# First loads of the modulation's rows queued behind loads of h, with shifted ranks and one scaling moved to GpSimd

## The chip, the cores and the metric

The kernel runs on one core of a Trainium2 chip. The metric is device microseconds (us) of one execution. In the text PE is TensorE (matmul), DVE is VectorE, ACT is ScalarE, POOL is GpSimd, and SP is SyncE, which here only issues DMA transfers. All transfers of this kernel are issued from SP, one after the other, in the order of the program; a transfer that has to wait for something holds up those behind it in that queue.

## The reference

The input x has 128 sequences of 64 tokens with 256 values each (8192 tokens), and `cond_1024` has one row of 256 values for each sequence. Two layers follow one another:

```python
x = x + _L0_ffn_ref(_L0_cond_ref(cond_1024, x, W, b, alpha), clip_x, clip_down, w_gate, w_up, w_down)
x = x + _L1_ffn_ref(_L1_cond_ref(x, cond_1024[:, None, :], w_q, ..., w_ada, b_ada), weight, bias)
```

`_L0_cond_ref` is a gated recurrence over the 64 time steps. `_L0_ffn_ref` is a feed-forward block with values rounded to 8 bits: `h = silu(gate) * up` is rounded with one scale for the whole tensor, so its largest absolute value must be known before any of it can be used. `_L1_cond_ref` is a transformer block in hyperbolic space, modulated by the condition:

```python
ada = t_emb @ w_ada + b_ada
sh_msa, sc_msa, g_msa, sh_mlp, sc_mlp, g_mlp = jnp.split(ada, 6, axis=-1)
xn = layer_norm(logmap0(x))
xm = expmap0(xn * (1 + sc_msa) + sh_msa)          # then attention with 16 heads of 16 values
attn_t = g_msa * logmap0(attn_out)
x = mobius_add(residual, expmap0(attn_t))
xn = layer_norm(logmap0(x))
xm = expmap0(xn * (1 + sc_mlp) + sh_mlp)          # then two products, w_f1 and w_f2
ff_t = g_mlp * logmap0(ff)
return mobius_add(residual, expmap0(ff_t))
```

`_L1_ffn_ref` rounds its input in blocks of 32 to a 6-bit format and multiplies it by a weight.

## The kernel before, in words

**First phase (0 to about 301 us).** The scan runs over 64 steps. Beside it the weights are prepared, and the six modulation vectors of all 128 sequences are computed and stored to DRAM as `ada_d`, eight copies of each row. Then `h_chunk` computes h in 16 blocks of 512 tokens and stores it to `h_d` and `hr_d`. L556 to L561 take the largest absolute value and derive the scale `cu`; L561 is the last DVE instruction of the phase.

**Second phase, `fused`.** The 8192 tokens are 64 tiles of 128, two tiles are a pair, and four tiles are a group; there are 16 groups. The loop at the end of `fused` is a software pipeline over turns k from -5 to 18. In turn k it writes down:

- `tail(k)`: the sums and coefficients after attention of group k and after the MLP of group k-3 (`chain.tail`, from L790), then `comb.a` and `comb.m` (L835), which add the residual; `comb.a` also feeds the statistics (L732, L733) of the second normalisation;
- `norms(k)`: the normalisation coefficients (`chain.ln`; `rnln` and `lnaln` at L666), then `modulate` (L751 to L756) for the MLP of group k and for the attention of group k+5, and `clip_ball`, which scales each tile by `sur` (L653 on DVE, L655 on POOL; `CFG['su0']` and `CFG['su1']` name the engine for each of the four tiles of a group, V for DVE and G for POOL);
- `fp6(k-3)`, `mlp(k)` and `attention(k+5)`;
- `front(k+6)`: for each of two pairs it rounds h to 8 bits (`front.q8`, L655 with `hb`), casts it (L913, L915), multiplies (`front.mm`, L925), scales (`front.x1`, L928), adds x (`front.add`, L930, with `xr` from DRAM), and stores the result in `x1_d`. It also issues the load of h for a pair two further on (`load_h`), because there are two buffers `hl`.

**Rows of the modulation.** `load_ada(which, kind, n_, i)` loads rows of `ada_d` for tile i. `which` is 0 for attention and 1 for the MLP; `kind` 0 loads shift and scale together (256 KB), `kind` 2 the gate (128 KB). The tiles are called ada00, ada02, ada10 and ada12, with 2, 2, 2 and 4 buffers. Their memory, like all of the second phase's work tiles, is that of the first phase's tiles, so no such load can start before the first phase has ended. The two `hl` buffers lie elsewhere, and pairs 0 and 1 of h are loaded while the first phase still runs.

**Order.** The text of the program doesn't set the order on an engine. Each instruction gets a priority, and a planner with a simulated clock goes through them: on each engine the ready instruction with the smallest priority comes first. The priority is set by

```python
tc.cur_priority = base + (turn_[0] + LA) * TURN + RANK[name]
```

with TURN = 1800, so a difference of 1800 in `RANK` is a whole turn. `tc.issue_after(ins)` adds an edge: instructions on the same engine as `ins` that are written inside the block come behind `ins` in that engine's order; no semaphore is added.

Of the kernel before, what the change touches and what calls it, by code (L numbers as in the profile page):

```python
# [22 lines left out]
P = 128  # L23
B, T, D = 128, 64, 256
# [18 lines left out]
NG = NT // GN  # L43
AR = 8
TS = 4
CFG = {'rnd': 'S', 'ef': 8, 'hold': [3, 0], 'mk': 2, 'raw': 1, 'mv': 6, 'xs': 3, 'la': 3, 'sb': 7, 'qks': 'GGGG', 'deq': 'VV', 'first': 1000, 'hb': 2, 'q_h': 'P', 'q_x1': 'P', 'q_xr': 'P', 'q_ot': 'P', 'q_out': 'P', 'q_ada': 'P', 'room': [[0.3, 0.3, 0.55], [0.5, 0.4, 0.2]], 'qv': 64, 'p1': 'GVGVGVGV', 'x1': 3, 'u1': 16, 'u2': 6, 'qkv': 2, 'sq': 1, 'uT1': 2, 'uT2': 2, 'qM': 2, 'kT': 2, 'e': 4, 'oT': 1, 'yT': 1, 'hq': 2, 'hl': 2, 'xr': 1, 'ot': 2, 'ada00': 2, 'ada02': 2, 'ada10': 2, 'ada12': 4, 'dn': 1, 'qk': 2, 'sc': 2, 'ao': 1, 'ml': 1, 'fp': 1, 'mod0': 'GGGV', 'mod1': 'VVVV', 'sqm0': 'SSSS', 'sqm1': 'SSSS', 'su0': 'VVVV', 'su1': 'VGVG', 'q8': 'GGGGGG', 'hqc': 'SSSVVV', 'qm': 'SSSS', 'x1a': 'GV', 'gate0': 'GGGG', 'gate1': 'GGGG', 'yb': 'GG', 'va': 'GGGG', 'sqt': 'SSSS', 'sqg': 'SSSS', 'sqo': 'SSVS', 'f2e': 'SSSS', 'early': 0, 'q8f': 'VVVVVV', 'hqf': 'SSSVVV', 'fl': 1, 'un': 2, 'jsu': 1, 'LA': 5, 'LM': 3, 'tl': 6, 'ord': 1, 'xt': 3, 'q_xt': 'P', 'fill': {'x1a': 'V', 'mod0': 'V'}}
GT = 4
NGR = NTILE // GT

TURN = 1800  # L50
RANK = {"front.q8": -307, "front.cast": 756, "front.mm": -718, "front.x1": -1025, "front.add": 4029, "store.x1": 0, "a.turn": -1220, "a.hi": -574, "a.lo": -1296, "a.qkv": 62, "a.qkvcopy": -226, "a.sq": 2196, "a.nh": -44, "chain.h": -3529, "a.qk": -90, "a.va": -90, "a.turnq": -90, "a.qm": -1303, "a.kt": -1196, "a.sc": -90, "a.e": -1043, "a.av": -90, "a.raw": -1317, "a.o": 3284, "a.turno": 1510, "a.ot": -3205, "a.wo": 975, "a.proj": -2819, "m.turn": 1039, "m.hi": -1145, "m.lo": -1565, "m.mm": 1778, "m.dot": -447, "m.copy": 619, "m.a": -39, "f.max": -10785, "f.q": 4848, "f.rnd": -1723, "f.deq": 2715, "f.turn": 765, "f.yt": 4647, "f.mm": 799, "load.ot": 10309, "f.add": -562, "store.out": 280, "x2n": 2132, "own": -510, "load.xt": -607, "chain.su": 3853, "chain.full": -6602, "chain.cf": 576, "chain.ln": -2738, "chain.tail": -2264, "stats1": 1285, "stats2": -440, "load.mod0": -1393, "load.mod1": -1624, "mod0.0": -3294, "mod0.1": -93, "mod0.2": 1311, "mod0.3": -3168, "mod1.0": 783, "mod1.1": 2701, "mod1.2": -5645, "mod1.3": 364, "sqm0": 2144, "sqm1": -1459, "clip0": -3110, "clip1": -2110, "sqt0": 280, "sqt1": 156, "gate0": -1945, "gate1": 2506, "sqg0": -990, "sqg1": 7667, "xdot.a": -1630, "xdot.m": 1591, "load.h": -5461, "load.x": 0, "a.sqo": 1108, "load.gate0": 2524, "load.gate1": 3539, "comb.a": 778, "comb.m": -2779}


LA, LM = CFG["LA"], CFG["LM"]

# [19 lines left out]
def tile_kernel(ctx, tc, a, out):  # L75
# [70 lines left out]
    with ExitStack() as l0:  # L146
# [15 lines left out]
        with ExitStack() as sc_:  # L162
# [270 lines left out]
            for n in range(T // TS):  # L433
# [5 lines left out]
                for i in range(TS):  # L439
# [22 lines left out]
                    with tc.issue_after(lv.ins), tc.issue_after(ls.ins), tc.issue_after(lp.ins):  # L462
# [4 lines left out]
                        for q in range(2):  # L467
                            if t < CFG["hold"][q]:
                                continue
                            left[q] = [min(l, 0.0) + r for l, r in zip(left[q], CFG["room"][q])]  # L470
                            while min(left[q]) > 0:
# [25 lines left out]
        for b0 in range(0, B, NBB):  # L497
            for c in range(2):

                q8 = xp.tile([P, NBB, T], I8, name="q8", tag="q8")  # L500
                src = hsT[:, c, :, b0 : b0 + NBB].rearrange("p t b -> p b t")
                if b0 < CFG["qv"]:
                    V.tensor_scalar(q8, src, isx, None, ALU.mult)
# [16 lines left out]
        def h_chunk(pg, pu, j, at, dst):  # L520
# [3 lines left out]
            cnt[0] += 1  # L524
            if CFG["p1"][cnt[0] % 8] == "G":
                uv = fw.tile([P, GN], F32, name="uv", tag="uv")
# [34 lines left out]
        V.tensor_scalar(sdh, sd_bc, sh[:, 0:1], None, ALU.mult)  # L561

    fused(ctx, tc, a, out_tok, x_tok, locals())


def fused(ctx, tc, a, out_tok, x_tok, L):
    nc = tc.nc
    V, S, G_, PE = nc.vector, nc.scalar, nc.gpsimd, nc.tensor
# [6 lines left out]
    ada_d, h_d, hr_d, x1_d = (L[k] for k in ("ada_d", "h_d", "hr_d", "x1_d"))  # L575
# [11 lines left out]
    Q = {"P": nc.sync, "S": S, "G": G_}  # L587

    def move(key, out, in_):
        Q[CFG["q_" + key]].dma_start(out=out, in_=in_)  # L590

    at = [0]
    turn_ = [-LA]
# [2 lines left out]
    def step(name):  # L596

        tc.cur_priority = base + (turn_[0] + LA) * TURN + RANK[name]

# [37 lines left out]
    def big(tag, shape, dt=F32):  # L637
        return pl.tile(shape, dt, name=tag, tag=tag, bufs=CFG[tag])
# [96 lines left out]
    def load_ada(which, kind, n_, i):  # L735

        t = big(f"ada{which}{kind}", [P, n_, D])
        o = (3 * which + kind) * D
        rows = ada_d[2 * i : 2 * i + 2, :, o : o + n_ * D].rearrange("s r d -> (s r) d")
        move("ada", out=t, in_=rows.unsqueeze(1).broadcast_to((2 * AR, T // AR, n_ * D)))  # L740
        return t

    def modulate(src, nm, aa, which, i0, u, un):

        for g in range(GT):
            step(f"load.mod{which}")
            ss = load_ada(which, 0, 2, i0 + g)
            step(f"mod{which}.{g}")
            ug = u[g]
            if pick(f"mod{which}", g) == "G":  # L750
                G_.tensor_scalar(ug, src[g], nm[:, g : g + 1], aa[:, g : g + 1], ALU.add, ALU.mult)  # L751
                G_.tensor_tensor(ug, ug, ss[:, 1, :], ALU.mult)
                G_.tensor_tensor(ug, ug, ss[:, 0, :], ALU.add)
            else:
                V.scalar_tensor_tensor(ug, src[g], nm[:, g : g + 1], ss[:, 1, :], ALU.add, ALU.mult)  # L755
                V.scalar_tensor_tensor(ug, ug, aa[:, g : g + 1], ss[:, 0, :], ALU.mult, ALU.add)  # L756
            step(f"sqm{which}")
            square_sum(pick(f"sqm{which}", g), f"u{which}", ug, un[:, g : g + 1])
# [78 lines left out]
    def two(p):  # L837
        return p.rearrange("p (i d) -> p i d", i=2)

    hls = []  # L840

    def load_h(pr):
        if pr >= NTILE // 2:
            return
        hl = ep.tile([P, 6, 2 * P], F32, name="hl", tag="hl", bufs=CFG["hl"])
        r = slice(pr // 2 % 2 * 64, pr // 2 % 2 * 64 + 64)
        ts = slice(pr % 2 * 2 * P, (pr % 2 + 1) * 2 * P)
        step("load.h")
        move("h", out=hl[:, 0:5, :], in_=h_d[pr // 2, :, :, ts].rearrange("j p t -> p j t"))
        move("h", out=hl[r, 5, :], in_=hr_d[pr // 4, r, ts])  # L850
        hls.append(hl)

    def runs(key, half):
# [39 lines left out]
    def front(i):  # L893
# [4 lines left out]
        for h2 in pairs:  # L898
# [12 lines left out]
            for e, r, j in runs("hqf" if early else "hqc", hs_):  # L911
                if e == "V":
                    V.tensor_copy(hq[r, j, :], q8[r, j, :])  # L913
                else:
                    S.copy(hq[r, j, :], q8[r, j, :])  # L915
            load_h(pr + CFG["hl"])
            step("load.x")
            xr = big("xr", [P, 2, D])
# [17 lines left out]
    def attention(i, u, sums):  # L936
# [124 lines left out]
        for h2 in pairs:  # L1061
            step("a.turno")
            pt = bank("ao")
            for i in range(2):
                for c in range(2):
                    o = (2 * i + c) * P
                    turn(pt[:, o : o + P], oall[2 * h2 + i][:, c * P : (c + 1) * P])
            oT = big("oT", [P, 4, P])
            step("a.ot")
            S.copy(oT.rearrange("p c t -> p (c t)"), pt)  # L1070
            step("a.wo")
            pm = bank("ao")
            for i in range(2):
                g = 2 * h2 + i
                for c in range(2):
                    PE.matmul(pm[:, i * D : (i + 1) * D], lhsT=oT[:, 2 * i + c, :], rhs=wo[:, c, :],
                              start=(c == 0), stop=(c == 1))
            for i in range(2):
                g = 2 * h2 + i
                step("a.proj")  # L1080
                V.scalar_tensor_tensor(av[g], pm[:, i * D : (i + 1) * D], full[:, g : g + 1], bo,
                                       ALU.mult, ALU.add)
                step("load.gate0")
                gb = load_ada(0, 2, 1, i0 + g)
                tail_sums(av[g], gb[:, 0, :], sums, g, 0, "a")
        return av

    def mlp(i, u, x2, sums):
# [36 lines left out]
        for g in range(GT):  # L1125
            step("m.a")
            V.scalar_tensor_tensor(av[g], u[g], cf[:, g : g + 1], bf2,  # L1127
                                   ALU.mult, ALU.add)
            step("load.gate1")
            gb = load_ada(1, 2, 1, i0 + g)  # L1130
            tail_sums(av[g], gb[:, 0, :], sums, g, 1, "m")
            x_dot(x2[g], av[g], sums, g, "m")
# [117 lines left out]
    for pr in range(CFG["hl"]):  # L1250
        load_h(pr)
# [67 lines left out]
```

## Time and profile before

| what | us |
|---|---|
| median of 3 runs | 1343.39 (1338.7 to 1350.01) |
| the profiled execution, its own time | 1340.01 |
| its span, first to last instruction | 1338.1 |
| PE busy | 1082.4 (81%) |
| DVE busy | 1098.6 (82%) |
| ACT busy | 848.2 (63%) |
| POOL busy | 840.5 (63%) |
| transferred | 163.64 MB, 122 GB/s over the span |

The 1.9 us between the span and the execution's own time lie before the first and after the last instruction. Busy shares are averages over stages: the first phase (to 301 us), the filling of the pipeline (to about 420 us), the steady turns (to about 1170 us, some 56 us each) and its emptying. In lines of a timeline the columns are start, length, engine (SPq is SP's issue queue), line of the kernel, operation, output and inputs, count, and in square brackets the idle time before it and what ended it. In lines of groups they are busy us and mean ns of one, then idle time. In a table of stretches each engine has its busy us and number of instructions, in the order PE, weight loads, DVE, ACT, POOL.

### The profile page before, as it was taken

How to read it: one execution, taken by the hardware profiler on the slowest of the kernel's cores; microseconds unless marked ns; L12 is line 12 of the kernel's file. 1: busy time of each engine (PE TensorE's matmuls, PEld its weight loads, DVE VectorE, ACT ScalarE, POOL GpSimd, SP SyncE). 2: the span in 40 equal slices, each digit the busy share in tenths (PEclk: the TensorE clock that was granted, in tenths of full speed). 3: DMA queues.
4: the chain of work that ended last, by engine and by line, in shares of the span. 5: the costliest groups of instructions: out<-in, count | busy, mean ns of one | idle time of the engine just before them, and what ended most of it. 6: DMA issues, size and time to landing. Idle time of an engine off the chain costs nothing.

```text
span 1338.1 us, 23886 instructions
## 1 busy us (share of the span) xinstructions
PE 1082.4 (81%) x7404; PEld 751.3 (56%) x7404; DVE 1098.6 (82%) x3337; ACT 848.2 (63%) x2607; POOL 840.5 (63%) x1024
## 2 busy tenths in 40 slices
PE   6999976984589798999887789796988989964453
PEld 5766642332356566666665566574765767653342
DVE  5776669995677889788989889899889897988774
ACT  2455547982368687877876667685767777754331
POOL 3110118865688868886896867867868766755552
PEclk9999979995589899987989889797978888886777
DMA  7722105678843315333234452414414222232211
GB/s 238 289 73 62 51 5 196 267 268 262 251 128 108 123 44 159 92 118 96 89 117 131 138 155 81 139 61 134 134 49 131 83 72 91 84 103 85 81 56 47
DMA packets 119304, 163.64 MB, mean 122 GB/s; under 512 B 10885, under 2 KB 72074, under 8 KB 119178
## 3 DMA queue, kind: packets, MB, share of 16 engines
q1 hardware_dynamic: 119178, 162.13, 37.8%
q8 instruction: 58, 0.95, 0.3%
q14 instruction: 68, 0.56, 0.1%
HBM read 115.94 MB, written 46.14 MB: 121 GB/s over the span
## 4 chain that ended last, share of the span: by engine, by line
DVE 36%; PE 27%; POOL 14%; DMA 8%; ACT 8%; issue 6%; SPq 0%; POOLq 0%; DVEq 0%; ACTq 0%
DMA ada<-ada_d 6%; PE pg L446 5%; PE qk L967 3%; PE pg L427 3%; DVE u L835 3%; DVE am L531 2%; PE sc L1024 2%; DVE hv L530 2%; DVE u L1127 2%; PE ao L1043 2%; DVE u L756 2%; DVE u L653 2%; DVE u L755 2%; PE ml L1112 2%; POOL qkv L994 2%
## 5 line engine op out<-in xcount | busy, mean ns | idle before, releaser
L644 ACT ACTIVATE junk<-u 128x256 bf16<-128x256 f32 x432 | 182.5, 425 | 128.0 <-POOL u L772 40.8
L967 PE MATMUL qk<-wqkv,uT 128*128 128x512 f32 (+1 forms) x768 | 181.2, 378 | 3.3 <-ACT uT L955 3.3
L772 POOL TENSOR_TENSOR u<-u,ada 128x256 f32<-128x256 f32 x128 | 101.4, 794 | 77.6 <-ACT junk L644 73.3
L1024 PE MATMUL sc<-qM,kT 64*64 64x256 f32 x1024 | 132.9, 442 | 13.3 <-ACT kT L1013 7.5
L967 PEld LDWEIGHTS qk<-wqkv,uT 128*128 128x128 f32 x768 | 127.7, 206 | 25.5 <-issue 6.8
L1043 PE MATMUL ao<-va,e 128*64 128x34 f32 x2048 | 95.8, 248 | 29.6 <-ACT e L1033 14.8
L1043 PEld LDWEIGHTS ao<-va,e 128*64 128x64 f32 x2048 | 84.3, 162 | 59.0 <-issue 17.2
L1112 PE MATMUL ml<-wm,uT 128*128 128x512 f32 (+1 forms) x384 | 113.6, 431 | 0.0
L651 ACT ACTIVATE qM<-sc,mhead 128x256 f32<-128x256 f32 x256 | 101.2, 490 | 9.2 <-PE sc L96 9.1
L1112 PEld LDWEIGHTS ml<-wm,uT 128*128 128x128 f32 x384 | 78.5, 208 | 43.1 <-issue 18.3
L925 PE MATMUL dn<-wdT,hq 128*128 128x256 bf16 (+1 forms) x384 | 68.9, 328 | 40.6 <-DVE x L928 17.3
L999 POOL TENSOR_TENSOR va<-qkv,comb 64x256 f32<-64x256 f32 x128 | 89.4, 715 | 11.2 <-PE ao L1043 8.7
L1024 PEld LDWEIGHTS sc<-qM,kT 64*64 64x64 f32 x1024 | 58.6, 150 | 55.0 <-issue 13.2
L1033 ACT ACTIVATE e<-sc 128x512 f32<-128x512 f32 x128 | 73.8, 598 | 24.0 <-PE sc L1024 19.0
L644 ACT ACTIVATION_READ_ACCUMULATOR junk<-u 128x1 f32 x432 | 86.6, 200 | 0.0
L994 POOL TENSOR_TENSOR qkv<-qkv,comb 128x512 f32<-128x512 f32 x64 | 71.8, 1134 | 18.9 <-DVE comb L985 10.7
L446 PE MATMUL pg<-hsT,WT 128*128 128x128 f32 x504 | 76.5, 293 | 8.5 <-ACT hsT L458 8.2
L446 PEld LDWEIGHTS pg<-hsT,WT 128*128 128x128 f32 x504 | 66.2, 195 | 26.9 <-ACT hsT L458 23.7
L655 POOL TENSOR_SCALAR hb<-hl,cu 128x1280 int8<-128x1280 f32 (+1 forms) x64 | 64.8, 1017 | 25.2 <-DMA hl<-h_d 14.3
L925 PEld LDWEIGHTS <-hq 128*128 128x128 bf16 (+1 forms) x384 | 39.2, 113 | 67.4 <-issue 23.4
L528 POOL TENSOR_TENSOR hv<-uv,sil 128x512 f32<-128x512 f32 x44 | 57.8, 1315 | 29.7 <-ACT sil L522 13.6
L975 DVE TENSOR_REDUCE nh<-sq 128x48 f32<-128x768 f32 x64 | 60.1, 939 | 17.1 <-ACT sq L973 16.8
(287 smaller groups left out, 3167.2 us busy)
## 6 DMA issues: line engine op xcount, KB each, us to landing
ada<-ada_d SPq DMA_DIRECT2D x128, 256.0 KB, 3.5
h_d<-hv SPq DMA_DIRECT2D x80, 256.0 KB, 2.3
hl<-h_d SPq DMA_DIRECT2D x32, 640.0 KB, 5.1
ada<-ada_d SPq DMA_DIRECT2D x128, 128.0 KB, 2.4
xt<-in_xT_dram SPq DMA_DIRECT2D x16, 512.0 KB, 3.7
xr<-in_x_dram SPq DMA_DIRECT2D x32, 256.0 KB, 4.0
x_d<-x SPq DMA_DIRECT2D x32, 256.0 KB, 2.7
xt<-x_d SPq DMA_DIRECT2D x32, 256.0 KB, 2.9
```

Source lines behind the costliest of these rows:

```text
L446: lp = PE.matmul(pg[c][:, st], lhsT=WT[:, k, c * P : (c + 1) * P], rhs=hp[:, k, :], start=False, stop=False, skip_group_check=True)
L644: S.activation(junk, src, AF.Square, accum_out=acc)
L651: S.activation(dst, src, AF.Copy, scale=by)
L772: ENG[pick(f"gate{which}", g)].tensor_tensor(av, av, gb, ALU.mult)
L925: PE.matmul(py[:, i * D : (i + 1) * D], lhsT=hq[r, j, i * P : (i + 1) * P], rhs=wdT[r, j, :], start=(i == 0 and j == 0), stop=(j == 5), sk ...
L967: PE.matmul(pm[:, :n_], lhsT=uT[:, z, k, cs], rhs=wqkv[:, w, k, lo:hi], start=False, stop=(k == 1 and q == 2))
L994: ENG[pick("qks", g)].tensor_tensor(qk, qk, bc_in(comb[:, xy * 48 : xy * 48 + 32], HD), ALU.mult)
L999: ENG[pick("va", g)].tensor_tensor(va[r, :, s, 0:HD], qkv[r, xy, 512:768].rearrange("p (h d) -> p h d", d=HD), bc_in(comb[r, xy * 48 + 32 ...
L1024: PE.matmul(sc[rr][s * T : (s + 1) * T, c * 256 : (c + 1) * 256].rearrange("p (v t) -> p v t", v=4), lhsT=kTs[xy][r, c, s * T : (s + 1) * ...
L1033: S.activation(e.rearrange("p c v t -> p (c v t)"), sc[rr], AF.Exp, scale=1.0 / math.sqrt(HD))
L1043: PE.matmul(pv[xy * T : (xy + 1) * T, hh], lhsT=E[2 * xy + hh // 4][:, c, hh % 4, :], rhs=vas[(2 * h2 + xy) % 4][:, c * 8 + hh], start=Tru ...
L1112: PE.matmul(pm[:, cs], lhsT=uT[:, z, k, i * P : (i + 1) * P], rhs=wm[:, w, k, cs], start=False, stop=(k == 1 and q == 2))
```

## The change

Three things are changed. `move` returns the instruction, `load_h` keeps a list `hlast` of the second load of each pair, and `load_ada` puts the first loads of each kind, as many as there are buffers, behind one of them: behind entry 1 for ada00, and behind the third last entry at that point of the program for the others. `su1` gives tile 0's scaling before the MLP to POOL instead of DVE. And 43 ranks are shifted.

```diff
-CFG = {..., 'su1': 'VGVG', ...}
+CFG = {..., 'su1': 'GGVG', ...}
...
     def move(key, out, in_):
-        Q[CFG["q_" + key]].dma_start(out=out, in_=in_)
+        return Q[CFG["q_" + key]].dma_start(out=out, in_=in_)
...
         rows = ada_d[2 * i : 2 * i + 2, :, o : o + n_ * D].rearrange("s r d -> (s r) d")
-        move("ada", out=t, in_=rows.unsqueeze(1).broadcast_to((2 * AR, T // AR, n_ * D)))
+
+        first = loaded[which, kind] = loaded.get((which, kind), -1) + 1
+        with tc.issue_after(hlast[1 if (which, kind) == (0, 0) else -3].ins) if first < CFG[f"ada{which}{kind}"] else nullcontext():
+            move("ada", out=t, in_=rows.unsqueeze(1).broadcast_to((2 * AR, T // AR, n_ * D)))
         return t
...
-    hls = []
+    hls, hlast, loaded = [], [], {}
...
-        move("h", out=hl[r, 5, :], in_=hr_d[pr // 4, r, ts])
+        hlast.append(move("h", out=hl[r, 5, :], in_=hr_d[pr // 4, r, ts]))
```

The ranks that move by more than 20 (smaller comes first):

| rank | shift |
|---|---|
| front.q8, front.cast, front.mm, front.add | +1891 |
| front.x1 | -2782 |
| all of attention (a.*), but for a.qkvcopy -795 and a.wo -614 | -841 |
| chain.h | +198 |
| chain.tail | -1477 |
| xdot.a | -4286 |
| comb.a, comb.m | +4153 |
| mod0.2 +282, store.out +221, m.dot -188, sqt0 -94, sqg1 -480 | |

More of the change, by code (lines that the diff above doesn't have):

```diff
@@ L45 @@
 TS = 4
-CFG = {'rnd': 'S', 'ef': 8, 'hold': [3, 0], 'mk': 2, 'raw': 1, 'mv': 6, 'xs': 3, 'la': 3, 'sb': 7, 'qks': 'GGGG', 'deq': 'VV', 'first': 1000, 'hb': 2, 'q_h': 'P', 'q_x1': 'P', 'q_xr': 'P', 'q_ot': 'P', 'q_out': 'P', 'q_ada': 'P', 'room': [[0.3, 0.3, 0.55], [0.5, 0.4, 0.2]], 'qv': 64, 'p1': 'GVGVGVGV', 'x1': 3, 'u1': 16, 'u2': 6, 'qkv': 2, 'sq': 1, 'uT1': 2, 'uT2': 2, 'qM': 2, 'kT': 2, 'e': 4, 'oT': 1, 'yT': 1, 'hq': 2, 'hl': 2, 'xr': 1, 'ot': 2, 'ada00': 2, 'ada02': 2, 'ada10': 2, 'ada12': 4, 'dn': 1, 'qk': 2, 'sc': 2, 'ao': 1, 'ml': 1, 'fp': 1, 'mod0': 'GGGV', 'mod1': 'VVVV', 'sqm0': 'SSSS', 'sqm1': 'SSSS', 'su0': 'VVVV', 'su1': 'VGVG', 'q8': 'GGGGGG', 'hqc': 'SSSVVV', 'qm': 'SSSS', 'x1a': 'GV', 'gate0': 'GGGG', 'gate1': 'GGGG', 'yb': 'GG', 'va': 'GGGG', 'sqt': 'SSSS', 'sqg': 'SSSS', 'sqo': 'SSVS', 'f2e': 'SSSS', 'early': 0, 'q8f': 'VVVVVV', 'hqf': 'SSSVVV', 'fl': 1, 'un': 2, 'jsu': 1, 'LA': 5, 'LM': 3, 'tl': 6, 'ord': 1, 'xt': 3, 'q_xt': 'P', 'fill': {'x1a': 'V', 'mod0': 'V'}}
+CFG = {'rnd': 'S', 'ef': 8, 'hold': [3, 0], 'mk': 2, 'raw': 1, 'mv': 6, 'xs': 3, 'la': 3, 'sb': 7, 'qks': 'GGGG', 'deq': 'VV', 'first': 1000, 'hb': 2, 'q_h': 'P', 'q_x1': 'P', 'q_xr': 'P', 'q_ot': 'P', 'q_out': 'P', 'q_ada': 'P', 'room': [[0.3, 0.3, 0.55], [0.5, 0.4, 0.2]], 'qv': 64, 'p1': 'GVGVGVGV', 'x1': 3, 'u1': 16, 'u2': 6, 'qkv': 2, 'sq': 1, 'uT1': 2, 'uT2': 2, 'qM': 2, 'kT': 2, 'e': 4, 'oT': 1, 'yT': 1, 'hq': 2, 'hl': 2, 'xr': 1, 'ot': 2, 'ada00': 2, 'ada02': 2, 'ada10': 2, 'ada12': 4, 'dn': 1, 'qk': 2, 'sc': 2, 'ao': 1, 'ml': 1, 'fp': 1, 'mod0': 'GGGV', 'mod1': 'VVVV', 'sqm0': 'SSSS', 'sqm1': 'SSSS', 'su0': 'VVVV', 'su1': 'GGVG', 'q8': 'GGGGGG', 'hqc': 'SSSVVV', 'qm': 'SSSS', 'x1a': 'GV', 'gate0': 'GGGG', 'gate1': 'GGGG', 'yb': 'GG', 'va': 'GGGG', 'sqt': 'SSSS', 'sqg': 'SSSS', 'sqo': 'SSVS', 'f2e': 'SSSS', 'early': 0, 'q8f': 'VVVVVV', 'hqf': 'SSSVVV', 'fl': 1, 'un': 2, 'jsu': 1, 'LA': 5, 'LM': 3, 'tl': 6, 'ord': 1, 'xt': 3, 'q_xt': 'P', 'fill': {'x1a': 'V', 'mod0': 'V'}}
 GT = 4
@@ L50 @@
 TURN = 1800
-RANK = {"front.q8": -307, "front.cast": 756, "front.mm": -718, "front.x1": -1025, "front.add": 4029, "store.x1": 0, "a.turn": -1220, "a.hi": -574, "a.lo": -1296, "a.qkv": 62, "a.qkvcopy": -226, "a.sq": 2196, "a.nh": -44, "chain.h": -3529, "a.qk": -90, "a.va": -90, "a.turnq": -90, "a.qm": -1303, "a.kt": -1196, "a.sc": -90, "a.e": -1043, "a.av": -90, "a.raw": -1317, "a.o": 3284, "a.turno": 1510, "a.ot": -3205, "a.wo": 975, "a.proj": -2819, "m.turn": 1039, "m.hi": -1145, "m.lo": -1565, "m.mm": 1778, "m.dot": -447, "m.copy": 619, "m.a": -39, "f.max": -10785, "f.q": 4848, "f.rnd": -1723, "f.deq": 2715, "f.turn": 765, "f.yt": 4647, "f.mm": 799, "load.ot": 10309, "f.add": -562, "store.out": 280, "x2n": 2132, "own": -510, "load.xt": -607, "chain.su": 3853, "chain.full": -6602, "chain.cf": 576, "chain.ln": -2738, "chain.tail": -2264, "stats1": 1285, "stats2": -440, "load.mod0": -1393, "load.mod1": -1624, "mod0.0": -3294, "mod0.1": -93, "mod0.2": 1311, "mod0.3": -3168, "mod1.0": 783, "mod1.1": 2701, "mod1.2": -5645, "mod1.3": 364, "sqm0": 2144, "sqm1": -1459, "clip0": -3110, "clip1": -2110, "sqt0": 280, "sqt1": 156, "gate0": -1945, "gate1": 2506, "sqg0": -990, "sqg1": 7667, "xdot.a": -1630, "xdot.m": 1591, "load.h": -5461, "load.x": 0, "a.sqo": 1108, "load.gate0": 2524, "load.gate1": 3539, "comb.a": 778, "comb.m": -2779}
@@ new lines @@
+RANK = {"front.q8": 1584, "front.cast": 2647, "front.mm": 1173, "front.x1": -3807, "front.add": 5920, "store.x1": 0, "a.turn": -2061, "a.hi": -1415, "a.lo": -2137, "a.qkv": -779, "a.qkvcopy": -1021, "a.sq": 1355, "a.nh": -885, "chain.h": -3331, "a.qk": -931, "a.va": -931, "a.turnq": -931, "a.qm": -2144, "a.kt": -2037, "a.sc": -931, "a.e": -1884, "a.av": -931, "a.raw": -2158, "a.o": 2443, "a.turno": 669, "a.ot": -4046, "a.wo": 361, "a.proj": -3660, "m.turn": 1039, "m.hi": -1145, "m.lo": -1565, "m.mm": 1778, "m.dot": -635, "m.copy": 619, "m.a": -39, "f.max": -10785, "f.q": 4848, "f.rnd": -1723, "f.deq": 2715, "f.turn": 765, "f.yt": 4647, "f.mm": 799, "load.ot": 10309, "f.add": -562, "store.out": 501, "x2n": 2132, "own": -510, "load.xt": -607, "chain.su": 3853, "chain.full": -6602, "chain.cf": 576, "chain.ln": -2738, "chain.tail": -3741, "stats1": 1285, "stats2": -440, "load.mod0": -1393, "load.mod1": -1624, "mod0.0": -3294, "mod0.1": -93, "mod0.2": 1593, "mod0.3": -3168, "mod1.0": 792, "mod1.1": 2710, "mod1.2": -5636, "mod1.3": 373, "sqm0": 2144, "sqm1": -1459, "clip0": -3110, "clip1": -2110, "sqt0": 186, "sqt1": 150, "gate0": -1945, "gate1": 2506, "sqg0": -999, "sqg1": 7187, "xdot.a": -5916, "xdot.m": 1591, "load.h": -5461, "load.x": 0, "a.sqo": 267, "load.gate0": 2524, "load.gate1": 3539, "comb.a": 4931, "comb.m": 1374}
```

## The prediction

> **What bounds the kernel now.** I read the page first, then the chain of waits in order of time, then a table of stretches, then the issue queue of SP. The page says that no single engine sets the end:
>
> ```profile
> PE 1082.4 (81%) x7404; PEld 751.3 (56%) x7404; DVE 1098.6 (82%) x3337; ACT 848.2 (63%) x2607; POOL 840.5 (63%) x1024
> ...
> DVE 36%; PE 27%; POOL 14%; DMA 8%; ACT 8%; issue 6%; SPq 0%; POOLq 0%; DVEq 0%; ACTq 0%
> ```
>
> The first line gives busy time, the second the shares of the chain that ended last. The 8% of DMA is the odd one: an average cannot say where it lies. The table of stretches (busy us of each engine, then granted PE clock, DMA share, GB/s) can:
>
> ```profile
> 300.00:320.00 20.00, 8.75 (x37) 4.47 (x38) 9.73 (x22) 3.33 (x4) 9.04 (x31) 0.50 0.77 223
> 320.00:340.00 20.00, 5.73 (x24) 2.92 (x23) 13.17 (x55) 6.16 (x21) 13.33 (x13) 0.50 0.96 294
> 340.00:360.00 20.00, 9.95 (x37) 5.97 (x38) 14.04 (x39) 5.60 (x18) 11.39 (x14) 0.50 0.91 262
> ...
> 500.00:600.00 100.00, 92.41 (x745) 65.46 (x742) 86.87 (x271) 78.05 (x250) 82.35 (x102) 0.93 0.41 125
> ...
> 900.00:1000.00 100.00, 81.75 (x605) 60.74 (x604) 92.86 (x284) 67.19 (x213) 73.16 (x86) 0.83 0.34 106
> ```
>
> From 301 us, where the scan's products are done, to about 360 us the fused loop fills: DMA runs at 0.77 to 0.96 of its time while PE idles. Later, DVE (87 to 93 us in 100) and PE share the bound. In the fill the chain runs over transfers:
>
> ```profile
> 305.66 9.32 DMA hl<-h_d
> ...
> 319.69 5.28 DMA xr<-in_x_dram
> ...
> 334.05 6.86 DMA ada<-ada_d
> ...
> 351.85 5.37 DMA ada<-ada_d
> ```
>
> In the SP queue at that point, rows of ada stand ahead of and around the h loads:
>
> ```profile
> 301.12 1.21 SPq L590 DMA_DIRECT2D ada<-ada_d  x2
> 302.38 0.58 SPq L590 DMA_DIRECT2D xr<-in_x_dram  x1
> 303.01 1.80 SPq L590 DMA_DIRECT2D ada<-ada_d  x3
> 305.08 0.95 SPq L590 DMA_DIRECT2D hl<-h_d  x2
> ...
> 308.38 1.24 SPq L590 DMA_DIRECT2D ada<-ada_d  x2
> ...
> 312.05 4.12 SPq L590 DMA_DIRECT2D ada<-ada_d  x3
> ```
>
> Ten loads: four of 256 KB and six of 128 KB by the sizes of the DMA view. Those are exactly the first loads that find their buffers free: ada00 2, ada10 2 (256 KB), ada02 2, ada12 4 (128 KB).
>
> **Part 1, the edges on the loads.** No instruction is added: an edge only fixes a place in SP's order. For ada00 it is `hlast[1]`, the load for pair 1. For the others `hlast[-3]`: when the gate rows of attention 0 are written in the program, four h loads exist, so it is pair 1 again; when ada10 and ada12 come (turn 0) fourteen exist, so it is pair 11. Pair 1's load was issued at 221.93 to 223.07, and the first ada load only at 301.12, released by L561. So for ada00 and ada02 the edge asks for what is there already: worth 0. What moves are 2 x 256 KB and 4 x 128 KB, 1.05 MB, from 301 to 316 us to behind pair 11's load, which the queue shows at 352.42.
>
> At the mean rate of 300 to 360 us, (223 + 294 + 262)/3 = 260 GB/s, 1.05 MB is 4.0 us of transfer. How much is on the path? Ahead of the h loads of 305.08 stand 3 x 256 and 2 x 128 KB; at least 512 KB (ada00) must stay, and 256 KB if the two small ones are ada02. So 256 to 512 KB leave from ahead of the 9.32 us wait: 1.0 to 2.0 us. The rest stood behind those h loads, and the next pair is issued at 317.34, where the DMA share has fallen to 0.56 (316 to 318 us in a finer table): little is gained there. Against it, the 1.05 MB comes back after 352, where the share is 0.8 to 1.06 until 364 and the chain waits for ada00 (5.37 us above): up to 4.0 us lost. The consumers of the moved rows bear no risk: the first DVE instruction that takes ada10 is at 482.7, 130 us after pair 11's load. Behind the moved loads in SP's order stand x stores, xr and ada00 loads; six issues at 0.52 us each, 3 us, hold them back once. I take **-1 us**, range -4 to +4.
>
> **Part 2, su1 from VGVG to GGVG.** One of four scalings per turn, 16 in all, goes from DVE to POOL.
>
> ```profile
> L653 DVE TENSOR_SCALAR u<-u,sur 128x256 f32<-128x256 f32 x96 | 41.5, 491 | 2.9 <-POOL sur L681 2.9
> ...
> L655 POOL TENSOR_SCALAR u<-u,sur 128x256 f32<-128x256 f32 x32 | 18.2, 576 | 0.8
> ```
>
> DVE gives up 16 x 0.43 (41.5/96) to 16 x 0.49 us = 6.9 to 7.9 us; POOL takes on 16 x 0.576 = 9.2 us, and it was 63% busy. But the turn of the first pair needs tiles 0 and 1, and before these ran side by side on two engines; now both queue on POOL. That is one POOL instruction more of latency, up to 0.576 us a turn, hidden while PE has attention work, bare in the drain (after 1170 us, where PE waits 32.9 us in all for L653). Taking half of DVE's 7 us as on the path in the steady turns (DVE holds 36% of the chain, the most of any), -3.5, and 0.5 us in three drain turns, +1.5: **-2 us**, range -7.9 to +9.2 (all 16 bare).
>
> One row warns of this edit: L653 takes between 0.334 and 1.415 us, median 0.346, so something stretches it at times. The Trainium skill names a candidate: by its page "GPSIMD Engine Reference", section 1 Specifications, GpSimd shares its SBUF interfaces with VectorE and contends with some DVE instructions, so work given to POOL can come back as slower work on DVE. If that held for the whole length of each moved instruction, DVE would lose 9.2 us for some 7 us given up, and this part would be +2 us instead of -2; the sum goes without it.
>
> **Part 3, the ranks.** A rank only decides which ready instruction an engine's order takes first (smaller first, 1800 to a turn). Front's q8, cast, mm and add go 1891 later, a whole turn; front.x1 2782 earlier; attention 841 earlier; chain.tail 1477 and xdot.a 4286 earlier; comb.a and comb.m 4153 later. Instructions and bytes stay the same; the trace has no row for an order that was not run, so I bound it by waits.
>
> In the fill: POOL, first turn, ran front work ahead of the coefficients of the first group:
>
> ```profile
> 343.55 0.30 POOL L679 TENSOR_SCALAR suq<-un 128x8 f32<-128x8 f32 x1 [1.88 <-ACT junk L644]
> 343.82 1.34 POOL L655 TENSOR_SCALAR hb<-hl,cu 128x1280 int8<-128x1280 f32 x1
> 345.12 1.27 POOL L930 TENSOR_TENSOR x<-x,xr 128x512 f32<-128x512 f32 x1
> 346.38 1.95 POOL L666 TENSOR_TENSOR sur<-suq,nhalf 128x8 f32<-128x8 f32 x1
> ```
>
> That is 1.34 + 1.27 = 2.6 us between suq and sur, 0.6 us (348.04, another hb) before L681, 1.3 us (321.88, hb) before rnln, and DVE's 1.4 us (331.3 to 332.7) between lnaln and its use: 5.9 us that a later front would free. The other bound: the front of later groups starts later by the same order, +6. I take -3.
>
> In the steady turns: an earlier chain.tail can shorten POOL's waits for its first DVE step, L790, 13.5 us in six waits between 420 and 1200. All of it would be -13.5; I take a third, **-4**. The loss that stands against it is the later comb.a, which opens norms of the same turn: 4 x (0.478 + 0.369 + 0.132) = 3.9 us a turn from L835, L732 and L733 (busy over count). While DVE has other work, that delay costs nothing, because attention is planned five turns ahead; with that cover gone it costs 3.9 us a turn, 62 us in 16 turns. I take 0 of it.
>
> **Sum.** -1 - 2 - 3 - 4 = -10 us. The profiled execution took 1340.01 us (span 1338.1 and 1.9 around it); it becomes 1330. The median of the runs is 1343.39, 3.4 above: **1333**, or 0.75% faster. About 1% (13.4 us) is what a measurement of this kernel can tell from no change.
>
> **Rivals.**
> A. *Most terms reach their good end.* -1 for loads, -7.9 for su1 (DVE wholly the bound), -5.9 in the fill, and half of 13.5, -6.7, in the turns: -21.5, 1322 us. For it: DVE at 93 of 100 us in the stretch 900:1000. Against it: PE at 82 to 92 in the same stretches, which gains nothing from su1. Chance of over 1% faster: 0.38.
> B. *comb.a comes too late (slower).* Place: tail(k) to norms(k), DVE. Price 3.9 us a turn. From three turns on it eats the 10 us; from (10 + 13.4)/3.9 = 6 turns it is over 1% slower; with seven, 1333 + 27 = 1360. For it: in the drain DVE is down to 75%, so nothing covers it there; chain.tail and xdot.a ahead of it move the other way, which is against. Chance of over 1% slower: 0.13.
> C. *The change does not do what it says.* Four of ten loads stay as shown; if the six others are no bottleneck and the ranks cancel, only su1's -2 stays: 1341. Chance 0.09, within 1%.
>
> **How the numbers follow.** Forecast 0.40 (1330 to 1341), C 0.09; the two fill the band within 1%: 0.49. A gives faster 0.38, B slower 0.13. Low end: -4 - 7.9 - 5.9 - 13.5 = -31, 1312. High end: the forecast with five turns of comb.a, 1333 + 19.5 = 1353, set at 1354; beyond it lies most of B. The forecast's own range is 1326 to 1342.
>
> **What the changed profile would show.** SP queue: at 301 us only four ada loads (2 x 256, 2 x 128 KB) ahead of the pair-2 h load, six more after pair 11's. The 9.32 us wait falls by 1 to 2 us. L653 x80, L655 on u x48, DVE's busy time down by about 7 us, POOL's up by 9. L666's sur and rnln of the first turn no longer stand behind hb. I would be wrong if the fill ends no earlier (first attention matmuls on qk at 354 us now) or if L755 and L756 for the next group wait long after L835.

## The result, and the profile after

The changed kernel is slower. Its median is 1353.51 us (1347.41 to 1357.66, 15 runs) beside 1343.76 us of the kernel before (1338.5 to 1350.01, 15 runs): a ratio of 1.0064 with an interval of [1.0047, 1.0082], some 9 us. The prediction said 1333. The profiled execution took 1350.6 us, its span is 1348.8.

The page of the kernel after, busy time of the engines and shares of the chain that ended last:

```profile
PE 1085.6 (80%) x7404; PEld 751.2 (56%) x7404; DVE 1102.6 (82%) x3321; ACT 850.4 (63%) x2607; POOL 848.2 (63%) x1040
...
DVE 36%; PE 26%; POOL 13%; DMA 9%; ACT 9%; issue 7%; SPq 1%; POOLq 0%; DVEq 0%; ACTq 0%
```

No engine has 10 us more work. The sixteen instructions that left DVE (3337 to 3321) arrived on POOL (1024 to 1040), and the shares of the chain are within a point of those before. POOL is busy 7.7 us longer, where 9 were forecast. DVE is busy 4.0 us longer, where 7 less were forecast; but its busy time also differs by 3.6 us between two executions of one and the same order (1098.6 before, 1102.2 in e5 below). The span grew by 10.7 us; the other 6.7 us of it DVE waits. The table of stretches of the kernel after (PE, weight loads, DVE, ACT, POOL, then clock, DMA share, GB/s):

```profile
300.00:320.00 20.00, 9.75 (x40) 5.12 (x41) 10.85 (x30) 3.63 (x6) 9.57 (x31) 0.51 0.68 202
320.00:340.00 20.00, 5.58 (x24) 2.81 (x22) 10.82 (x40) 5.05 (x15) 11.96 (x10) 0.50 0.90 270
340.00:360.00 20.00, 9.13 (x35) 5.14 (x36) 15.37 (x47) 5.74 (x19) 13.46 (x17) 0.50 0.77 229
360.00:380.00 20.00, 15.62 (x86) 10.91 (x85) 16.00 (x46) 12.32 (x32) 16.17 (x21) 0.93 0.91 255
```

The DMA share falls in each stretch up to 360 us (0.77, 0.96, 0.91 before) and rises in the fourth, from 0.56 to 0.91: that is the megabyte that moved, and the first phase, which ended 1.6 us later in this execution. SP's issue queue after:

```profile
302.73 1.21 SPq L589 DMA_DIRECT2D ada<-ada_d  x2
303.98 0.58 SPq L589 DMA_DIRECT2D xr<-in_x_dram  x1
304.61 1.16 SPq L589 DMA_DIRECT2D ada<-ada_d  x2
306.85 0.95 SPq L589 DMA_DIRECT2D hl<-h_d  x2
...
361.33 4.80 SPq L589 DMA_DIRECT2D ada<-ada_d  x6
```

Four loads of ada stay at the start, six stand at 361 us. The chain in order of time, its long transfers in the fill:

```profile
307.43 6.96 DMA hl<-h_d
...
319.62 5.85 DMA xr<-in_x_dram
...
335.21 6.29 DMA ada<-ada_d
343.26 5.57 DMA ada<-ada_d
...
358.95 9.59 DMA hl<-h_d
```

The first wait for h is 2.4 us shorter (9.32 before), and another one for h, 9.59 us, has come at the place where the six loads now stand in the queue. The fill ends no earlier: the first attention product starts at 357.4 us (356.6 before). Counted from the first load of rows, at 302.73 and 301.12 us, it is 0.8 us shorter.

### The profile page after: what moved, and what is told of

Same layout as the page of the kernel before. It is cut to its first block, busy times and chain, and to the rows that moved or that the text cites. A ratio compares the mean times of both kernels' runs of the same rounds, so it can differ in the third digit from the quotient of the medians.

```text
span 1348.8 us, 23878 instructions
## 1 busy us (share of the span) xinstructions
PE 1085.6 (80%) x7404; PEld 751.2 (56%) x7404; DVE 1102.6 (82%) x3321; ACT 850.4 (63%) x2607; POOL 848.2 (63%) x1040
## 4 chain that ended last, share of the span: by engine, by line
DVE 36%; PE 26%; POOL 13%; DMA 9%; ACT 9%; issue 7%; SPq 1%; POOLq 0%; DVEq 0%; ACTq 0%
DMA ada<-ada_d 6%; PE pg L445 5%; DVE u L837 3%; PE qk L969 3%; PE pg L426 3%; PE sc L1026 3%; DVE am L530 2%; POOL u L774 2%; DVE u L757 2%; DVE hv L529 2%; DVE junk L782 2%; DVE u L652 2%; ACT qM L650 2%; DVE u L758 2%; ACT junk L643 2%
## 5 line engine op out<-in xcount | busy, mean ns | idle before, releaser
L643 ACT ACTIVATE junk<-u 128x256 bf16<-128x256 f32 x432 | 182.8, 425 | 126.6 <-POOL u L774 41.5
L969 PE MATMUL qk<-wqkv,uT 128*128 128x512 f32 (+1 forms) x768 | 184.6, 383 | 3.4 <-ACT uT L957 3.4
L1114 PE MATMUL ml<-wm,uT 128*128 128x512 f32 (+1 forms) x384 | 117.1, 444 | 0.0
L1114 PEld LDWEIGHTS ml<-wm,uT 128*128 128x128 f32 x384 | 81.7, 215 | 41.8 <-issue 14.6
L654 POOL TENSOR_SCALAR hb<-hl,cu 128x1280 int8<-128x1280 f32 (+1 forms) x64 | 65.8, 1034 | 21.4 <-DMA hl<-h_d 10.6
L457 ACT ACTIVATE hsT<-gate 128x128 f32<-128x128 f32 x128 | 39.6, 309 | 54.2 <-DVE gate L456 54.2
```

Source lines behind the costliest of these rows:

```text
L643: S.activation(junk, src, AF.Square, accum_out=acc)
L969: PE.matmul(pm[:, :n_], lhsT=uT[:, z, k, cs], rhs=wqkv[:, w, k, lo:hi], start=False, stop=(k == 1 and q == 2))
L1114: PE.matmul(pm[:, cs], lhsT=uT[:, z, k, i * P : (i + 1) * P], rhs=wm[:, w, k, cs], start=False, stop=(k == 1 and q == 2))
```

## The experiments

Every time below stands beside runs of the kernel before on the same chip, so the ratio counts. These theories appear in the expectations: **O**, the loss is in what the ranks ask for; **E** or **D**, the moved transfers cost by themselves; **S**, the scaling on GpSimd costs by itself; **P**, an edit costs through the planner, which lays a new order on all engines; **X**, nearly any new order is slower than the one of before, whatever caused it (in the expectations of e1 to e4, X still says that any edit moves the time by 5 to 10 us, in either direction); **Q**, an edit's worth depends on the order laid for it.

### One part at a time

**e1_edges**: the edges alone, `RANK` and `su1` as before.

> Of the change only the edges on the first loads of ada; su1 and ranks as before. Theory O (the loss is in the ranks: comb.a comes later, chain.h and front move): the edges are worth -1 us as predicted, range -4 to +4, so 1340 to 1348 us beside a before of 1343.8. Theory E (the edges themselves cost, because six loads come back at 361 us, where DMA is busy for the rows of ada00): 1348 to 1354 us, most of the 9 us of the whole change. Theory X (the planner's order answers to any edit with some 5 to 10 us in either direction, whatever the edit means): clearly off in either direction, also where no transfer waits longer.

Measured: 1362.37 us, ratio 1.0153 [1.011, 1.0196]. The edges alone lose more than twice what the whole change loses.

**e2_su1**: one character.

```diff
-'su1': 'VGVG'
+'su1': 'GGVG'
```

> Of the change only su1 GGVG; no edges, ranks as before. Theory O: -2 us, range -8 to +9. Theory E: nothing measurable. Theory S (tile 0's scaling on GpSimd delays the turn of the first pair in the drain): +3 to +9 us, and PE's waits for the scaling of u before ml grow after 1170 us. Theory X: off by 5 to 10 us in either direction.

Measured: 1350.04 us, 1.0054 [1.0024, 1.0083].

**e3_ranks**: the ranks alone.

> Of the change only the 43 ranks; no edges, su1 as before. Theory O: 1350 to 1358 us, all of the loss is here. Theories E and S: no slower than before, 1336 to 1344 us. Theory X: off in either direction.

Measured: 1349.37 us, 1.0046 [1.002, 1.0072].

**e4_edges_su1**: edges and su1, ranks of before.

> Edges and su1 GGVG, ranks as before. Theory O: 1336 to 1344 us, for the ranks are what costs. Theories E and S: 1350 to 1358 us, as the whole change. Theory X: not the sum of the two single edits.

Measured: 1358.04 us, 1.0125 [1.0084, 1.0165].

Each part alone is slower, and they don't add up: 1.53 + 0.54 + 0.46 is 2.5%, the whole is 0.64%. Theory O is gone: with the edges and su1 in place, the new ranks win back 0.6%. But these four can't tell E and S from P, since each edit also lets the planner lay a new order. The edges alone give a different order on every engine (on DVE, a diff of the two records that e5 and e6 below pin, of 3129 entries each, has 2354 lines).

### The order pinned

In the next kernels the order on each engine is recorded from one kernel and imposed on another, by an edge from each instruction to the one before it in that record:

```python
def pin(tc, nc):
    traced = nc.cur_bb.bb.instructions
    for seq in json.loads(zlib.decompress(base64.b85decode(ORDER))):
        for a, b in zip(seq, seq[1:]):
            tc.add_manual_dep(traced[b], traced[a].name, mybir.DependencyInfo(
                mybir.DependencyClass.NoSync, mybir.DependencyReason.DATA), reason="pin")
```

**e5_loads_moved_order_kept**: record of before, six loads moved in SP's record (12 lines of difference, all on SP).

> The order of the kernel before is pinned instruction by instruction on every engine; only the six first loads of ada10 and ada12 stand later in SP's order, behind the loads for pair 12, where the kernel with the edges alone has them. Theory D (the moved transfers cost by themselves, as rows of ada00 wait for them): the 20 us of the edges alone stay, 1357 to 1365 us. Theory P (the edge costs through the planner: a load that comes later in its simulated time gives another order on all engines): the transfers are worth what was predicted for them, -1 us within -4 to +4, so 1339 to 1348 us.

Measured: 1340.81 us, 1.0002 [0.9978, 1.0026]. The place isn't quite that of e1: in e5's trace the six loads are issued behind pair 11's load (353.7 us) and ahead of pair 12's (363.9), in e1's at 360.2 to 364.2 us, behind pair 12's (357.3). That is one pair earlier in the queue, in the same stretch of time.

**e6_order_of_edges_loads_back**: the reverse.

> The order of the kernel with the edges alone is pinned on every engine, but the six loads stand in SP's order where they were before the change. Theory D: the loss goes, 1340 to 1348 us. Theory P: the loss stays, 1357 to 1366 us.

Measured: 1363.02 us, 1.0179 [1.0152, 1.0205].

In e5's trace the instructions of DVE, ACT and POOL follow one another as in the kernel before, without a difference. No kernel pins the old order and changes nothing else, but e5, and e7 below (1.0002 and 0.9988), leave little room for a cost of pinning itself.

This pair settles the edges. Kernels e1 and e5 have the same instructions and load the same rows late, one pair apart; e1 loses 1.5%, e5 nothing. Kernel e6 has e1's order, loads them early as the kernel before does, and loses 1.8%. Theory D falls by e6 above all, P holds. The table of the stretch 420 to 1170 us (PE, weight loads, DVE, ACT, POOL) and the view of the line of the attention's first products, of the kernel before:

```profile
420.00:1170.00 750.00, 659.38 (x5249) 483.67 (x5247) 659.80 (x2060) 548.59 (x1772) 563.48 (x684) 0.88 0.34 107
```

```profile
L967 PE MATMUL qk<-wqkv,uT x768: 275/389/987, 356.6 to 1122.9; 128*128 128x512 f32 x157, 128*128 128x256 f32 x35
```

of e5:

```profile
420.00:1170.00 750.00, 656.07 (x5218) 479.16 (x5217) 658.98 (x2056) 545.79 (x1763) 560.60 (x682) 0.88 0.34 106
```

```profile
L969 PE MATMUL qk<-wqkv,uT x768: 276/388/987, 357.8 to 1123.6; 128*128 128x512 f32 x157, 128*128 128x256 f32 x35
```

of e1:

```profile
420.00:1170.00 750.00, 653.00 (x5123) 470.98 (x5123) 648.02 (x2009) 537.02 (x1718) 546.47 (x664) 0.88 0.33 102
```

```profile
L969 PE MATMUL qk<-wqkv,uT x768: 276/390/987, 355.8 to 1151.6; 128*128 128x512 f32 x158, 128*128 128x256 f32 x34
```

and of the changed kernel:

```profile
420.00:1170.00 750.00, 653.85 (x5176) 478.12 (x5174) 651.73 (x2019) 543.79 (x1747) 561.79 (x686) 0.88 0.34 105
```

```profile
L969 PE MATMUL qk<-wqkv,uT x768: 276/392/984, 357.4 to 1135.3; 128*128 128x512 f32 x164, 128*128 128x256 f32 x28
```

All four start attention within 2 us of each other. The last product comes at 1122.9 and 1123.6 in the order of before, at 1135.3 in the changed kernel, and at 1151.6 in e1; from there to the end of the span it is 215, 215, 214 and 207 us. So the loss is complete before the pipeline empties, and it gathers after attention has started. A part may lie before 420 us: from 301 us to there PE has done 464 products in the changed kernel and in e1, 515 before and 530 in e5. It doesn't grow evenly: the 673rd of the 768 weight loads for these products starts at 1046.4 us in the changed kernel and at 1047.0 before, the last at 1135.1 and 1122.7. Other work stands at other places in the new order, so this row alone doesn't say where the loss arises. Between 420 and 1170 us DVE idles for 750 - 659.8 = 90 us and 91 us in the old order, 98 us in the changed kernel and 102 us in e1, with less of its work done by 1170 us (2019 and 2009 instructions where 2060 were done before). DVE's idle time isn't the whole story: in e8 below it is busy for 660.35 us of this stretch, as before, with 2029 instructions done, and the kernel loses 1.7%.

**e7_su1_order_kept**: record of before; each of the sixteen scalings moves from DVE's record to POOL's, ahead of tile 1's.

> The order of the kernel before is pinned; only the sixteen scalings of tile 0 before the MLP go from DVE to GpSimd, each directly ahead of tile 1's scaling. Theory P: the edit alone is worth what was predicted, -2 us, range -8 to +3, so 1336 to 1347 us. Theory S (the serial pair of scalings delays the first turn, and holds DVE's port): +4 to +9 us, 1348 to 1353 us, as the edit measured with a new order.

Measured: 1339.35 us, 0.9988 [0.9964, 1.0011]. Theory S falls as well: -1.6 us by the ratio, beside -2 predicted; the interval takes in no difference.

**e9_edits_order_kept**: both edits in the order of before.

> The order of the kernel before is pinned; in it the six loads stand later on SP and the sixteen scalings of tile 0 run on GpSimd: the two edits that the engines see, without a new order. Theory P (the loss of the change is in the new order): no slower than before, the sum of the two single edits, 1337 to 1344 us. The rival, that the two edits together cost something that neither shows alone: 1348 us and more.

Measured: 1338.39 us, 0.997 [0.9947, 0.9992], some 4 us faster. This is faster than both kernels, if by little. What the engines are asked to do differently is worth what Parts 1 and 2 of the prediction said, -3 us. And since e9 and the changed kernel have the same instructions, and the six loads late (in e9 as in e5, one pair earlier), what parts them, 0.997 and 1.0064, is the order.

**e10_order_of_after_edits_undone**: the changed kernel's order, with loads and scalings as before.

> The order of the changed kernel is pinned on every engine, but the six loads stand where they were before the change and tile 0 is scaled on DVE again. Theory P: the whole loss stays, 1350 to 1358 us. The rival, that the edits cost and not the order: 1341 to 1346 us.

Measured: 1367.08 us, 1.0196 [1.017, 1.0222]. The loss stays in the order of after, as P says, but the time is 9 us above the upper end of what was expected. Undoing the edits made the kernel slower still (1.0196 beside 1.0064), so an edit of little worth in one order can be worth much in another. The next two part them.

**e13_order_of_after_loads_back** and **e14_order_of_after_su1_back**: the same order, one edit undone in each.

> The changed kernel's order is pinned and tile 0 stays on GpSimd; only the six loads stand early again. Theory P with edits that keep their small worth in any order: 1350 to 1358 us, as the changed kernel. Theory Q (the loads' place matters in the order that was laid for it, since fill and h loads then collide): 1358 to 1368 us.

> The changed kernel's order is pinned and the loads stay late; only tile 0's scaling is on DVE again, directly ahead of tile 2's. If the scalings are what cost in e10 (sixteen more instructions on DVE at a place where the turn of tile 0 waits for them): 1358 to 1368 us. If the loads are: 1350 to 1358 us.

Measured: 1354.29 us, 1.0077 [1.0049, 1.0104], and 1365.39 us, 1.0154 [1.0119, 1.0188]. The place of the loads is worth nothing in this order either (1.0077 beside 1.0064, intervals overlapping); tile 0's scaling on DVE accounts for the added loss. The place it got on DVE, directly ahead of tile 2's, was chosen by hand, so this shows what such an instruction costs at an unfitting place, not what the planner would have made of it.

### Is any new order slower?

**e8_edges_two_pairs_later**: the edges behind another h load.

```diff
-hlast[1 if (which, kind) == (0, 0) else -3]
+hlast[1 if (which, kind) == (0, 0) else -1]
```

> As the edges alone, but behind the last h load written down at that point instead of the third last: pair 13 instead of pair 11 for the MLP's rows, pair 3 instead of pair 1 for the gates of attention 0. Theory D: the same loss or a little less, 1355 to 1365 us. Theory P: another order, so a time that has nothing to do with the place of the loads, anywhere from 1343 to 1370 us.

Measured: 1360.33 us, 1.0173 [1.014, 1.0207]. Taken alone this suits D as well as P; e5 and e6 rule D out.

**e11_idle_memset**: the kernel before with an idle instruction.

```diff
             h0T = setup.tile([P, 2, B], F32, name="h0T")
+            V.memset(h0T, 0.0)
```

> The kernel before with one DVE memset of 128x256 values at the very start, overwritten by the load of h0T that now waits for it; its own cost is under 1 us. The planner gives another order from there on (half of DVE's rows change place). Theory X (before has an order picked for speed, and nearly any other order is slower): +5 to +20 us, 1348 to 1363 us. Rival (only what the change means to the planner costs, for example h loads ahead of rows): same as before, 1341 to 1346 us.

Measured: 1352.5 us, 1.008 [1.0057, 1.0104].

**e15_second_idle_edit**: another one.

```diff
         V.reciprocal(cu, sh[:, 0:1])
+        V.reciprocal(cu, sh[:, 0:1])
```

> The kernel before with the reciprocal of the scale cu taken twice (0.17 us by its row, on the path once). The planner gives another order for the second phase. Theory X (nearly any other order is slower than the one of before): 1348 to 1365 us. Rival (the memset of e11 cost in another way): 1341 to 1346 us.

Measured: 1354.89 us, 1.008 [1.0042, 1.0118].

Two edits that mean nothing, the one of under a microsecond and the other of 0.17 us, cost 11 us each, about as much as the change under study. The loss isn't at their own place: the first load of rows is issued at 298.77 us in e11 and at 302.51 in e15 (301.12 before). In both, DVE works less between 420 and 1170 us, 645.08 and 643.39 us, beside 659.80 of the kernel before. The stretch in e11 and in e15:

```profile
420.00:1170.00 750.00, 643.31 (x5196) 466.59 (x5203) 645.08 (x2031) 544.16 (x1754) 555.79 (x676) 0.90 0.34 106
```

```profile
420.00:1170.00 750.00, 638.22 (x5079) 464.48 (x5081) 643.39 (x2010) 537.64 (x1720) 550.72 (x672) 0.90 0.34 104
```

What these two share with the change under study, by the text of the programs, is that each moves something in the planner's simulated time. Theory X holds for all eight new orders that were laid: e1 to e4, e8, e11, e15 and the changed kernel are slower by 0.46 to 1.73%. Why the order of before is a fast one no run shows.

**e12_after_comb_ranks_back**: the changed kernel with the old ranks of comb.a and comb.m.

> The whole change, but comb.a and comb.m with the ranks of before (4153 smaller). The slower rival of the prediction (comb.a comes too late): the loss goes, 1340 to 1346 us, and stats2 and the next norms start sooner after L837. Theory X: another order again, no way back to 1343; 1346 to 1365 us.

Measured: 1351.59 us, 1.0071 [1.0043, 1.0098]. No way back, but not by another order, as theory X would have it: in the trace of e12 the instructions of DVE, ACT and POOL and the loads on SP follow one another exactly as in the changed kernel. So the shift of 4153 in these two ranks changes nothing that the engines see, and can't be the cause here; why it changes nothing the runs don't show. As a time, e12 is the changed kernel run again (1.0071 beside 1.0064).

### What in the new orders costs

DVE's waits between 420 and 1170 us, of the kernel before (waiting line, line waited for, us in total, times, longest):

```profile
DVE nh L975 <- ACT sq L973: 14.3, 10, 2.6
DVE u L755 <- DMA ada<-ada_d: 13.2, 13, 3.1
...
DVE satc L796 <- POOL r L666: 3.0, 5, 1.7
...
DVE pz L709 <- POOL rnln L666: 2.4, 4, 0.8
...
DVE junk L780 <- POOL u L772: 2.2, 3, 1.4
```

and after:

```profile
DVE u L757 <- DMA ada<-ada_d: 12.6, 13, 2.9
DVE junk L782 <- POOL u L774: 8.5, 11, 1.6
DVE nh L977 <- ACT sq L975: 7.8, 9, 1.3
DVE satc L798 <- POOL r L665: 7.2, 4, 3.5
DVE pz L721 <- ACT l1qln L720: 5.4, 6, 2.1
...
DVE pz L708 <- POOL rnln L665: 4.0, 4, 1.5
```

Some waits shrink (nh), others grow: those for the small coefficients (satc 3.0 to 7.2, rnln 2.4 to 4.0) and for the gate products on POOL (junk 2.2 to 8.5). DVE takes its instructions in the order laid down (e5's trace has the pinned order without a difference), so a coefficient that comes late holds up what stands behind it. That is a reading of two traces; no run took such a wait away by itself, and no single row has the 9 us.

POOL's waits between 420 and 1200 us show the same exchange. The second row is the one from which the prediction took its -4 us. Before:

```profile
POOL u L772 <- ACT junk L644: 58.7, 36, 5.9
...
POOL r L666 <- DVE q L790: 13.5, 6, 5.3
```

and after:

```profile
POOL u L774 <- ACT junk L643: 68.5, 37, 4.7
...
POOL r L665 <- DVE q L792: 3.9, 3, 1.8
```

One wait shrinks by 9.6 us, another grows by 9.8.

The granted clock is a candidate for a part of the loss in the changed kernel's order. Its mean is 0.860 over the changed kernel's 15 runs and 0.857 to 0.859 in e10, e12, e13 and e14, which have nearly that order; in the runs of the kernel before beside the experiments it is 0.872 to 0.874. Among the 23 runs of the kernel before beside e5, a straight line through time against clock falls by 5.0 us for each 0.01 of clock. By an estimate from these numbers some 6 of the 9 us would go with the clock. No run shows whether the lower clock makes the time or only comes with it. And it isn't what new orders cost in general: e1, e6, e11 and e15 lose 0.8 to 1.8% at clocks of 0.871, 0.872, 0.876 and 0.879. Which part of the order costs what stays open.

## Why the prediction was wrong, point by point

- **Part 1, the edges.** The transfers were read rightly in the main. Four of the ten loads stayed, six moved (behind pair 12's load, not pair 11's). The 9.32 us wait fell by 2.4 us, in e5 too (6.88), where 1 to 2 were said, though only one load fewer stands ahead of it, four where there were five. The loss that "comes back after 352" is there as the 9.59 us wait. Net, e5: 1.0002 [0.9978, 1.0026], beside -1 us. What failed is the sentence "No instruction is added: an edge only fixes a place in SP's order". With the edges the planner lays another order on every engine. That was worth some +20 us in e1 and +24 in e6, and had no term in the sum.
- **Part 2, su1.** L652 x80, L654 x48, -1.6 us in e7 beside -2: right, with the order kept. With a new order the same character costs 0.54% (e2). The contention that the prediction cites (the Trainium skill, "GPSIMD Engine Reference", section 1 Specifications) would have made this part +2 us, a ratio of 1.0015; the interval of e7 ends at 1.0011, just below. In e7 the 80 scalings left on DVE take 35.6 us, 6 less than the 96 before (41.5); in the changed kernel they take 41.2. What stretches them there no run shows. The rows of e7, then of the changed kernel:

```profile
L652 DVE TENSOR_SCALAR u<-u,sur 128x256 f32<-128x256 f32 x80 | 35.6, 501 | 2.3 <-POOL sur L680 2.2
```

```profile
L652 DVE TENSOR_SCALAR u<-u,sur 128x256 f32<-128x256 f32 x80 | 41.2, 564 | 2.5 <-POOL sur L680 2.5
```

- **Part 3, the ranks.** This is the step of the sum that failed. -3 for the fill and -4 for the turns were taken from waits that a better order could shorten, as if a wait that shrinks shortened the kernel. In the fill, hb (1.34 us) and x (1.26 us) still stand on POOL between suq at 344.29 and sur at 347.50 in the changed kernel, as before. In the turns, POOL's wait for L790 did fall, from 13.5 to 3.9 us, more than the third that was taken, and the kernel became no faster, as other waits grew. By the runs, the new order costs 1.0064/0.997 = 1.0094, +12.6 us, where -7 stood. The ranks by themselves have no one worth that could be added to a sum: alone they cost 0.46%, 6 us (e3); laid over the other two edits they win some 8 us (e4 to the changed kernel, 1.0125 to 1.0064).
- **The rivals.** A needed all terms at their good ends. B had the right sign, but the later rank of comb.a on which it rests changes no order (e12). Nor is its sign there, a longer wait of L755 and L756 after L835: L757, which is L755 of before, still waits for rows of ada, 12.6 us beside 13.2. C was right on the four loads and wrong on the total. The range, 1312 to 1354, held the time by its upper edge only, and by luck: that edge stands for five turns of B's delay.
- **The sum** -1 - 2 - 7 = -10 would have been -3 without the term for the order, and e9 measured -4. The error, some 20 us, is in the assumption that a new order costs nothing or helps.

## What to carry to other kernels

Where a planner lays the order, an edit has two prices: what it asks of the engines and queues, which can be summed from rows of the profile, and the new order, which can't. Part them on the chip by pinning the old order under the new content and the new order under the old; here that turned a 0.6% loss into a 0.3% gain. A wait that an edit shortens is no gain until the time says so: here one of 13.5 us shrank by 9.6, and the kernel became slower. And before an edit is blamed or praised for some tenths of a percent, try an edit that means nothing: if that moves the time as much, as here, the old order was a good one among those that the planner can lay, and the edit has not been priced yet.

## What the runs showed that was not expected

- Two orders of the same instructions differ by 2%: e10 has the instructions of the kernel before and the loads where they were, and takes 1367 us beside 1342. A part of this comes from the sixteen scalings on DVE, whose place was chosen by hand (e14).
- The same sixteen scalings, 0.35 us each by their median on DVE, were worth nothing measurable in one order (e7) and some 0.9% in another (e14 beside the changed kernel, 1.0154/1.0064), 12 us for 16 x 0.35 = 5.5 us of work, at a place on DVE that was chosen by hand.
- Freeing 1.05 MB from the most loaded stretch of the transfers, at shares up to 0.96, gained nothing (e5). In the changed kernel's chain of the fill the first wait for h is 2.4 us shorter, and a wait of 9.59 us for another load of h has come.
